# Where the products are added: onto the image in SBUF, or onto the output in DRAM

## The chip, the cores and the metric

The kernel runs on one core of a Trainium2 chip. The metric is device time in microseconds (us) of one execution; several runs are taken and their median is given. The core's engines are named as in the profile: PE is TensorE, DVE is VectorE, ACT is ScalarE, POOL is GpSimd and SP is SyncE, which only issues transfers.

## What is computed

The input has 160 images of 128 channels and 32 x 32 pixels in float32. Each is group-normalised, convolved 3 x 3 with weights that are quantised from U (five sets of weights; image number modulo 5 chooses the set), and added to the unnormalised image:

```python
def reference(x, L0_conv_U):            # x (160, 128, 32, 32), U (5, 128*128*9)
    beta, alpha = U.max(), U.min()
    s1 = (beta - alpha) / 3.0
    v1 = s1 * floor(U / s1)
    s2 = s1 / 5.0
    v2 = s2 * floor((U - v1) / s2)
    w = (v1 + v2).reshape(128 * 5, 128, 3, 3)
    g = x.reshape(160, 32, 4, 32, 32)   # 32 groups of 4 channels
    n = ((g - mean(g)) / sqrt(var(g) + 1e-5)).reshape(x.shape)
    act = grouped_conv(n.reshape(32, 5 * 128, 32, 32), w, groups=5, pad=1)
    return x + act.reshape(x.shape)
```

An image is 512 KB: 128 partitions (channels) with one row of 4 KB (1024 pixels) each.

## The kernel before

**Images and buffers.** The images are worked through set by set, 32 of one set after another. Two neighbouring images make a chunk of 1 MB (`NB = 2`), and a ring of ten chunks (`CHUNKS = 10`, tile `xt`) holds them in SBUF. `load(c)` brings a chunk in on SyncE's queue.

**Work on one image.** ACT or DVE measures it (`measure`, L377 and L384 on ACT), five images make a group whose means and variances are finished by small matmuls and a few short instructions (`ngm`, `twice`, `rstd`). Most images, 120, are "combined": DVE and POOL form sums and differences of neighbouring columns (`v`, lines 829, 836, 817 and 850), ACT scales them to float16 (`vh`, L879), and DVE forms the remainder (`vl`, L885). The 33 "plain" ones and a few at the start go through `z`, `hi` and `lo` instead. These are the last readers of the image in `xt`, but for its own addition at the end. PE then multiplies (L929, L984), with ACT and DVE exchanging partial sums (`leave` L1021, `pairs` L1030 and L1032), and leaves the products of an image in a pair of PSUM banks (`eo`, two buffers).

**The addition.** `residual(i)` ends an image, in one of two ways. By hand (`by_hand`: the first three images, the last four, and every tenth from 24 to 154) DVE adds `eo` onto the image in SBUF (L1073). For the other 139, ACT copies `eo` into one of three buffers `sum` (L1056), and `accumulate(i)` lets POOL issue a transfer that adds `sum` onto the image (L1079):

```python
self.nc.gpsimd.dma_start(self.image(i), self.sum.pop(i), accum_op=ALU.add)
```

When both images of a chunk are complete, SyncE stores the chunk (L1084). The next load into that buffer waits for that store. The last four images are stored one by one (L1075, L1066).

**The order of work.** Nearly all of it stands in a timetable, `steady`. Each step becomes a job with an engine, a cost and the jobs it needs; `Timetable.run` simulates the engines, picks for DVE and ACT the job that is due first, and the instructions are emitted in the order of the simulated starts. The order on PE is given, but for small matmuls that are slipped in. Stores and loads are jobs of an engine "queue" that takes 10 us each; they are emitted on SyncE's queue where the timetable starts them, and SyncE works through its queue in order: a transfer that has to wait holds up all that stand behind it. The same is true of POOL, whose queue holds the `v`, `z`, powers and accumulates.

Of the kernel before, what the change touches and what calls it, by code (L numbers as in the profile page):

```python
# [11 lines left out]
ALU = mybir.AluOpType  # L12
# [9 lines left out]
NB = 2  # L22
LAST = 4
# [23 lines left out]
class Timetable:  # L47
# [15 lines left out]
    def add(self, kind, engine, cost, emit, needs=(), **kw):  # L63
        job = Job(kind, engine, cost, emit, [n for n in needs if n is not None], **kw)
        self.jobs.append(job)
        place = {"tensor": self.tensor, "small": self.small, "beside": self.beside}
        place.get(engine, self.others).append(job)
        return job
# [452 lines left out]
class Main:  # L521
# [22 lines left out]


    CHUNKS = 10
    STEADY = 7
    BY_VECTOR = (8, 10, 11, 14, 19, 24, 29, 34)
    PLAIN = (9, 13, 17, *(22 + 9 * k + d for k in range(15) for d in (0, 4)))
# [11 lines left out]
    def __init__(self, tc, ctx, keep, x, u, out):  # L561
        self.tc = tc
        nc = self.nc = tc.nc
        self.imgs, C, self.H, self.W = x.shape
        P = self.P = nc.NUM_PARTITIONS
        assert C == P and self.H * self.W == 1024
        self.per_set = self.imgs // N_SETS
        self.xv = x.rearrange("(b n) c h w -> n c b (h w)", n=N_SETS)
        self.ov = out.rearrange("(b n) c h w -> n c b (h w)", n=N_SETS)
        self.uv = u.rearrange("n (o i k) -> n o i k", o=C, k=TAPS)  # L570

        def pool(name, bufs, **kw):
            return ctx.enter_context(tc.tile_pool(name=name, bufs=bufs, **kw))

        self.const = pool("const", 1)
        self.qpool = pool("quant", 1)
        self.wpool = pool("weights", 2)
        self.upool = pool("u", 1)
        self.xpool = pool("x", self.CHUNKS)
        self.zpool = pool("z", 2)  # L580
        self.parts = pool("parts", 4)
        self.rows = pool("rows", 4)
        self.wide = pool("wide", 3)
        self.wide_parts = pool("wide_parts", 4)
        self.evac = pool("evac", 2)
        self.sums = pool("sums", 3)
        self.unread = pool("unread", 1)
        self.small = pool("small", 5)
        self.ps_eo = pool("ps_eo", 2, space=PSUM)
        ps_m = pool("ps_m", 1, space=PSUM)  # L590
        ps_small = pool("ps_small", 1, space=PSUM)
        self.steps = Steps(nc, keep)

        self.m1a, self.m1b, self.m2_ps = (
            ps_m.tile([P, self.H // 2, self.W], F32, tag=name, name=name)
            for name in ("m1a", "m1b", "m2")
        )
        self.pair = [self.m1a, self.m2_ps]

        small = ps_small.tile([P, 512], F32, tag="small", name="small")  # L600
        self.pt, self.pg = small[:, : ROW * P].rearrange("p (k o) -> p k o", k=ROW), small[:, ROW * P :]
        self.chunks, self.z, self.hi, self.v, self.eo, self.m2 = {}, {}, {}, {}, {}, {}
        self.sum = {}
        self.turn_of = {}
        turn = 1
        for i in range(self.FIRST, self.imgs):
            if not self.plain(i):
                self.turn_of[i], turn = turn, 1 - turn
        self.tables, self.wts, self.across = {}, {}, {}
        self.columns = []  # L610

        cuts = [0, 2, 4, 8, 12, 16, *range(20, self.imgs + 1, 5)]
        self.groups = [range(a, b) for a, b in zip(cuts, cuts[1:])]
        self.group_of = {i: k for k, g in enumerate(self.groups) for i in g}
        self.stats = {}
# [432 lines left out]
    def residual(self, i):  # L1048

        nc = self.nc  # L1050
        eo = self.eo.pop(i)
        del self.hi[i]
        n, b = self.place(i)
        if not self.by_hand(i):
            self.sum[i] = self.sums.tile([self.P, 1024], F32, tag="sum", name=f"sum{i}")
            nc.scalar.copy(self.as_banks(i, self.sum[i]), self.flat(i, eo))  # L1056
            return
        xj = self.image(i)
        if i == self.imgs - 1:
            image, banks = self.as_banks(i, xj), self.flat(i, eo)  # L1060
            for a, quarters in ((0, (slice(0, 512),)), (1, (slice(0, 256), slice(256, 512)))):
                for h, q in enumerate(quarters):
                    nc.vector.tensor_add(image[:, a, q], banks[:, a, q], image[:, a, q])
                    if a == 1:
                        half = slice(h * 512, h * 512 + 512)
                        nc.sync.dma_start(self.ov[n, :, b, half], xj[:, half])  # L1066
            return
        image = self.as_banks(i, xj)
        if eo is self.pair:
            for a in range(2):  # L1070
                nc.vector.tensor_add(image[:, a], self.bank(eo, a), image[:, a])
        else:
            nc.vector.tensor_add(image, self.flat(i, eo), image)  # L1073
        if i >= self.imgs - LAST:
            nc.sync.dma_start(self.ov[n, :, b], xj)  # L1075

    def accumulate(self, i):
        if i in self.sum:
            self.nc.gpsimd.dma_start(self.image(i), self.sum.pop(i), accum_op=ALU.add)  # L1079

    def store(self, i):
        if 0 <= i < self.imgs - LAST and i % NB == NB - 1:
            n, b = self.place(i)
            self.nc.sync.dma_start(  # L1084
                self.ov[n, :, b - NB + 1 : b + 1, :], self.chunks[i // NB]
            )

    def run(self):
        nc, P = self.nc, self.P
# [126 lines left out]
        self.steps.choose()  # L1216
        for c in range(6, self.CHUNKS):
            self.load(c)
        for i in range(self.FIRST):
# [26 lines left out]
            self.residual(j)  # L1246
        self.steady(12, self.CHUNKS)

    def steady(self, measured, loaded):

        nc, imgs, first = self.nc, self.imgs, self.FIRST
        self.vector_engine = nc.vector.engine
        table = Timetable()
        add = table.add
        images = range(first, imgs)


        main, m1, m2, at, t = {}, {}, {}, {}, 0.0
# [3 lines left out]
        chain = [i for i in images if not self.plain(i)]  # L1262
# [27 lines left out]
        wide, beside, high, low, left, pairs, out, whole = ({} for _ in range(8))  # L1290
# [37 lines left out]


        stores, loads = {}, {}  # L1330
        for c in range(imgs // NB):
            if (c + 1) * NB <= imgs - LAST:
                stores[c] = add("store", "queue", 10.0, lambda c=c: self.store(c * NB + 1), (
                    [whole.get(c * NB + j) for j in range(NB)]
                ))
            if c >= loaded:
                loads[c] = add("load", "queue", 10.0, lambda c=c: self.load(c), (stores.get(c - self.CHUNKS),))


        combs = [i for i in images if self.combined(i)]  # L1340
        for n, i in enumerate(combs):
            if n >= 3:
                for job in (wide[i], beside[i]):
                    job.after(low[combs[n - 3]])
            if n >= 4:
                high[i].after(main[combs[n - 4]][1])
        plains = [i for i in images if self.plain(i) or i == 6]
        for a, b in zip(plains, plains[1:]):
            beside[b].after(low[a])
            high[b].after(main[a][1])  # L1350
        for n, i in enumerate(chain):
            if i in low and n >= 4:
                low[i].after(main[chain[n - 4]][1])
            if n >= 1 and i > first + 1:
                m2[i].after(left[chain[n - 1]])
            if n >= 2 and i > first + 1:
                m1[i].after(pairs.get(chain[n - 2]))
            if n >= 3:
                left[i].after(pairs.get(chain[n - 2]))
            if i in m2:  # L1360
                m2[i].after(low.get(i))
                main[i][0].after(pairs[i])
            if n and i in low and chain[n - 1] in pairs:
                pairs[chain[n - 1]].after(low[i])
        for i in images:
            if self.plain(i):
                main[i][0].after(low[i])
            user = main[i][0] if self.plain(i) else pairs.get(i)
            if user and i - 2 in out:
                user.after(out[i - 2])  # L1370
            if i - 3 in out:
                out[i].after(whole[i - 3])


        last_ve = None
# [1 line left out]
        for g, group in enumerate(self.groups):  # L1377
# [3 lines left out]
            for i in group:  # L1381
                if i < measured:
                    continue
                load = loads.get(i // NB)
# [27 lines left out]
        for n in range(1, N_SETS):  # L1412
# [3 lines left out]
            if n > 1:  # L1416
                load = add("load u", "queue", 0.1, lambda n=n: self.load_set(n), (last_rest,), ready=at[use - 40])
# [11 lines left out]
            for k, (kind, cost, gen) in enumerate(steps):  # L1429
                ready = start + (end - start) * k / len(steps)  # L1430
                job = add("step", kind, cost, lambda gen=gen: next(gen), (last,), ready=ready, late=ready + 6.0)
# [19 lines left out]
        for job in done:  # L1451
            for other in job.with_it:
                before = self.before_last()
# [58 lines left out]
```

## Time and profile before

| | |
|---|---|
| runs | 985.06, 990.72, 983.9 us; median 985.06 |
| profiled execution: own time / span | 983.48 / 981.7 us |
| PE busy | 938.0 us (96%) |
| DVE, ACT, POOL busy | 921.0 (94%), 852.4 (87%), 517.8 us (53%) |
| loads (1 MB each) | 78, median 7.6 us from issue to landing |
| stores (1 MB each) | 78, median 5.7 us |
| accumulates (512 KB each) | 139, 0.898 us of POOL each, median 6.8 us to landing (4.5 to 12.2) |
| DMA engines | 48.1% loads and stores, 39.7% accumulates |
| HBM | 89.19 MB read, 83.89 MB written |

An engine's busy time is the sum of its instructions' durations; idle time of an engine costs something only if another one waits for it. The DMA shares are the time that packets of a queue took, as a share of the 16 DMA engines' time over the span. "To landing" is from a transfer's issue to its end. In the views, a bracket or an arrow `<-` names what released an engine that had been idle.

### The profile page before, as it was taken

The page shows a single profiled execution, that of the slowest core. Times are in us where ns is not written, and L with a number is a line of the kernel's source. Part 1 is how long each engine was busy: PE and PEld are TensorE (multiplying, and loading weights), DVE is VectorE, ACT ScalarE, POOL GpSimd, SP SyncE. Part 2 cuts the span into 40 slices and gives each one's busy share as a digit, 9 for nine tenths or more (in the row PEclk, how much of TensorE's full clock was granted, in tenths as well). Part 3 has the DMA queues.
Part 4 walks back from the last instruction along what each step waited for, and adds up shares of the span by engine and source line. Part 5 has one row for each costly group of instructions (what it writes and reads, how often), then busy time and mean ns, then how long its engine had stood idle before and what let it go on. Part 6 is the DMA issues. An engine that isn't in the chain of part 4 may idle for free.

```text
span 981.7 us, 13015 instructions
## 1 busy us (share of the span) xinstructions
PE 938.0 (96%) x4514; PEld 442.2 (45%) x4514; DVE 921.0 (94%) x1175; ACT 852.4 (87%) x1118; POOL 517.8 (53%) x495
## 2 busy tenths in 40 slices
PE   2889999989999999999999999999999999999996
PEld 1434444444444444444444444444444444444443
DVE  7999999989999999899999999999999898978985
ACT  5779989869899997999999899998999999999651
POOL 4234655635575456465545557455655556455540
PEclk9999999999999999999999999999999999999999
DMA  9526999897999989999999889899999999897765
GB/s 354 219 86 195 239 265 291 229 283 211 260 286 271 263 254 241 277 269 263 254 319 268 241 235 275 242 278 306 249 277 257 257 255 283 250 299 218 182 166 196
DMA packets 65403, 246.89 MB, mean 252 GB/s; under 512 B 5040, under 2 KB 5040, under 8 KB 65328
## 3 DMA queue, kind: packets, MB, share of 16 engines
q1 hardware_dynamic: 45312, 173.09, 48.1%
q0 software_dynamic: 20016, 72.88, 39.7%
q8 instruction: 37, 0.61, 0.2%
q14 instruction: 38, 0.31, 0.1%
HBM read 89.19 MB, written 83.89 MB: 176 GB/s over the span
## 4 chain that ended last, share of the span: by engine, by line
PE 44%; DVE 31%; DMA 8%; issue 7%; ACT 6%; POOL 3%; SPq 0%; DVEq 0%; POOLq 0%; ACTq 0%
PE eo L984 15%; PE eo L929 13%; DVE vl L885 8%; PE m L984 7%; DVE v L829 5%; PE m1b L984 4%; PE m1a L984 4%; DMA xt<-in_x_dram 3%; DVE v L836 3%; DVE eo L1032 3%; DVE eo L1030 3%; DMA xt<-sum 3%; DVE lo L892 2%; ACT vh L879 2%; DMA out_dram<-xt 1%
## 5 line engine op out<-in xcount | busy, mean ns | idle before, releaser
L885 DVE SCALAR_TENSOR_TENSOR vl<-v,rstd,vh 128x2048 f16<-128x2048 f32 x120 | 286.3, 2386 | 23.5 <-ACT vh L879 23.2
L984 PE MATMUL eo<-vh,wt 128*128 128x512 f16 x720 | 269.5, 374 | 0.3 <-DVE eo L1032 0.2
L984 PE MATMUL eo<-vl,wt 128*128 128x512 f16 x720 | 269.6, 374 | 0.0
L879 ACT ACTIVATE vh<-v,rstd 128x2048 f16<-128x2048 f32 x120 | 239.0, 1995 | 23.1 <-POOL v L850 10.8
L817 POOL TENSOR_SCALAR v<-xt,ngm 128x64 f32<-128x64 f32 x120 | 129.6, 1080 | 212.8 <-issue 114.1
L984 PEld LDWEIGHTS <-across 128*128 128x128 f16 x1440 | 140.9, 98 | 172.0 <-issue 9.6
L984 PEld LDWEIGHTS <-wt 128*128 128x128 f16 x1488 | 145.2, 100 | 160.3 <-DVE rows L914 1.8
L929 PEld LDWEIGHTS <-wt 128*128 128x128 f16 x1368 | 134.0, 99 | 156.8 <-DVE eo L1032 3.3
L929 PE MATMUL eo<-hi,wt 128*128 128x496 f16 (+3 forms) x702 | 186.9, 377 | 4.8 <-DVE eo L1032 2.6
L377 ACT ACTIVATE junk<-xt 128x1024 uint8<-128x1024 f32 x152 | 160.5, 1056 | 26.5 <-DMA xt<-in_x_dram 24.9
L384 ACT ACTIVATE junk<-xt,mv 128x1024 uint8<-128x1024 f32 x152 | 174.4, 1148 | 2.8
L929 PE MATMUL eo<-lo,wt 128*128 128x496 f16 (+2 forms) x630 | 166.6, 375 | 0.0
L1079 POOL DMA_DIRECT2D xt<-sum x139 | 123.0, 898 | 78.5 <-ACT sum L1056 50.4
L1056 ACT COPY sum<-eo 128x1024 f32<-128x1024 f32 x139 | 148.3, 1067 | 16.8 <-PE eo L984 10.4
L850 POOL TENSOR_TENSOR v<-xt 128x512 f32<-128x512 f32 x120 | 155.6, 1297 | 0.0
L829 DVE TENSOR_TENSOR v<-xt 128x960 f32<-128x960 f32 x120 | 145.1, 1209 | 0.1
L984 PE MATMUL m<-vl,across 128*128 128x512 f16 x360 | 134.8, 375 | 4.4 <-DVE vl L885 4.4
L984 PE MATMUL m<-vh,across 128*128 128x512 f16 x360 | 134.9, 375 | 2.4 <-ACT m L1021 2.4
L856 POOL TENSOR_SCALAR z<-xt,ngm,rstd 128x1024 f32<-128x1024 f32 x33 | 60.8, 1841 | 65.0 <-DVE vl L885 16.9
L836 DVE SCALAR_TENSOR_TENSOR v<-xt,twice 128x512 f32<-128x512 f32 x120 | 91.3, 761 | 0.0
L1021 ACT ACTIVATE m<-m 128x512 f32<-128x512 f32 x124 | 73.5, 593 | 19.7 <-PE m L984 13.7
L422 POOL TENSOR_TENSOR rstd<-ve,mhalf 128x5 f32<-128x5 f32 (+2 forms) x34 | 54.3, 1598 | 54.2 <-DVE v L829 34.0
(143 smaller groups left out, 1001.3 us busy)
## 6 DMA issues: line engine op xcount, KB each, us to landing
xt<-in_x_dram SPq DMA_DIRECT2D x78, 1024.0 KB, 7.6
out_dram<-xt SPq DMA_DIRECT2D x78, 1024.0 KB, 5.7
xt<-sum POOLq DMA_DIRECT2D x139, 512.0 KB, 6.8
u<-in_L_conv_U_dram SPq DMA_DIRECT2D x4, 576.0 KB, 6.0
xt<-in_x_dram SPq DMA_DIRECT2D x4, 512.0 KB, 10.1
range<-in_L_conv_U_dram SPq DMA_DIRECT2D x3, 576.0 KB, 8.3
out_dram<-xt SPq DMA_DIRECT2D x3, 512.0 KB, 3.0
u<-in_L_conv_U_dram SPq DMA_DIRECT2D x2, 288.0 KB, 3.1
```

Source lines behind the costliest of these rows:

```text
L377: self.nc.scalar.activation(junk, image, ACTF.Copy, scale=-1.0 / image.shape[1], accum_out=self.mv[:, j, 0:1],)
L384: self.nc.scalar.activation(junk, image, ACTF.Square, bias=self.mv[:, j, 0:1], accum_out=self.mv[:, j, 1:2],)
L817: return self.nc.gpsimd.tensor_scalar(self.view(self.v[i], 0, (512 + W // 2 - 1, 2), (W // 2, H)), self.view(self.image(i), 1, (W - 3, 2), ...
L829: nc.vector.tensor_tensor(self.view(v, 1, (511, 2), (half, H), (1, half - 1)), self.view(x, 1, (1, 2), (W, H), (2, half - 1)), self.view(x ...
L836: nc.vector.scalar_tensor_tensor(v[:, 1024:1536], even, st.twice[:, j], odd, ALU.add, ALU.add)
L850: return [self.outer_columns(i), self.nc.gpsimd.tensor_sub(self.v[i][:, 1536:], odd, even)]
L879: self.nc.scalar.mul(vh, self.v[i], st.rstd[:, j])
L885: yield self.nc.vector.scalar_tensor_tensor(vl, self.v[i], st.rstd[:, j], self.hi[i], ALU.mult, ALU.subtract)
L929: nc.tensor.matmul(self.bank(target, a)[:, first:end, c0:c1], self.wts[n, col][:, k, :], tile[:, s0 : s0 + 2 * (end - first) - 1 : 2, c0 + ...
L984: self.nc.tensor.matmul(out, weights, moving, start=start and j == 0, stop=False, skip_group_check=True)
L1056: nc.scalar.copy(self.as_banks(i, self.sum[i]), self.flat(i, eo))
L1079: self.nc.gpsimd.dma_start(self.image(i), self.sum.pop(i), accum_op=ALU.add)
```

## The change

Each image that isn't summed by hand is stored to the output unchanged, as soon as it is loaded (`store_input`): a whole chunk at once, or one image where the other is summed by hand. `accumulate(i)` then adds the products onto that place of the output in DRAM, after the store has landed. A load into a buffer of the ring waits for the last readers of the old images and for their early store, and no longer for an accumulate and a store behind it. Images by hand are added in SBUF as before and stored one by one. The timetable counts 14 us for a load or store instead of 10; the four new constants `WIDE, HIGHS, ROWS, SUMS` have the values that stood in the code before.

```diff
     CHUNKS = 10
+    LANDING = 14.0
+    WIDE, HIGHS, ROWS, SUMS = 3, 4, 4, 3
...
         else:
             nc.vector.tensor_add(image, self.flat(i, eo), image)
-        if i >= self.imgs - LAST:
-            nc.sync.dma_start(self.ov[n, :, b], xj)
+        self.store(i)
 
     def accumulate(self, i):
-        if i in self.sum:
-            self.nc.gpsimd.dma_start(self.image(i), self.sum.pop(i), accum_op=ALU.add)
+        n, b = self.place(i)
+        added = self.nc.gpsimd.dma_start(self.ov[n, :, b], self.sum.pop(i), accum_op=ALU.add)
+        self.after(added, self.stored[i].ins)
 
     def store(self, i):
-        if 0 <= i < self.imgs - LAST and i % NB == NB - 1:
-            n, b = self.place(i)
-            self.nc.sync.dma_start(
-                self.ov[n, :, b - NB + 1 : b + 1, :], self.chunks[i // NB]
-            )
+        n, b = self.place(i)
+        return self.nc.sync.dma_start(self.ov[n, :, b], self.image(i))
+
+    def store_input(self, c):
+        images = [i for i in range(c * NB, c * NB + NB) if not self.by_hand(i)]
+        if len(images) == NB:
+            n, b = self.place(images[0])
+            stored = self.nc.sync.dma_start(self.ov[n, :, b : b + NB, :], self.chunks[c])
+            self.stored.update((i, stored) for i in images)
+            return
+        self.stored.update((i, self.store(i)) for i in images)
...
         stores, loads = {}, {}
+        def readers(i):
+            found = [beside.get(i), wide.get(i)]
+            return found + [out[i]] if i in out and self.by_hand(i) else found
         for c in range(imgs // NB):
-            if (c + 1) * NB <= imgs - LAST:
-                stores[c] = add("store", "queue", 10.0, lambda c=c: self.store(c * NB + 1), (
-                    [whole.get(c * NB + j) for j in range(NB)]
+            both, before = (range(k * NB, k * NB + NB) for k in (c, c - self.CHUNKS))
+            if c >= loaded:
+                loads[c] = add("load", "queue", self.LANDING, lambda c=c: self.load(c), (
+                    [stores.get(c - self.CHUNKS), *(j for i in before for j in readers(i))]
                 ))
-            if c >= loaded:
-                loads[c] = add("load", "queue", 10.0, lambda c=c: self.load(c), (stores.get(c - self.CHUNKS),))
+            if not all(self.by_hand(i) for i in both):
+                stores[c] = add(
+                    "store", "queue", self.LANDING, lambda c=c: self.store_input(c),
+                    (loads.get(c), loads.get(c + 1)), ready=6.0 * c if c < loaded else 0.0,
+                )
+            for i in both:
+                if not self.by_hand(i):
+                    whole[i].after(stores[c])
```

## The prediction

> **What bounds the kernel now.** I read the busy shares first, then stretches of the span, then the queues.
>
> ```profile
> PE 938.0 (96%) x4514; PEld 442.2 (45%) x4514; DVE 921.0 (94%) x1175; ACT 852.4 (87%) x1118; POOL 517.8 (53%) x495
> ```
>
> TensorE is busy for 938.0 of 981.7 us, so 43.7 us is all that a change which takes no matmul away can give back. The table of stretches says where those are.
>
> ```profile
> 0.00:25.00 25.00, 6.23 (x20) 3.43 (x21) 19.70 (x45) 12.95 (x24) 10.48 (x26) 1.00 0.94 355
> ...
> 200.00:250.00 50.00, 45.65 (x221) 21.53 (x222) 44.67 (x56) 40.36 (x53) 25.70 (x24) 1.00 0.87 243
> ...
> 400.00:450.00 50.00, 47.42 (x227) 21.96 (x225) 47.80 (x55) 47.58 (x65) 25.13 (x22) 1.00 0.92 257
> ...
> 700.00:750.00 50.00, 50.00 (x243) 23.67 (x242) 48.74 (x60) 47.89 (x63) 29.67 (x26) 1.00 0.97 264
> ```
>
> The first busy time in a row is PE's, the last three columns are granted clock, DMA share and GB/s. Before 75 us PE idles 25.4 us, after 960 us 8.1 us: start and end, in instructions that the change leaves alone. From 75 to 960 us the rows add up to 874.4 busy of 885, so **10.6 us is the whole prize in the steady part**. The last column but one is the warning: the DMA engines are 0.92 to 0.97 busy beside a full PE.
>
> Next, who waits for transfers: all waits, then the DMA queue's own.
>
> ```profile
> ACT junk L377 <- DMA xt<-in_x_dram: 24.9, 8, 8.2
> SPq L1084 <- DMA xt<-sum: 476.0, 75, 15.8
> SPq L635 <- DMA out_dram<-xt: 338.8, 56, 11.1
> ```
>
> SyncE's queue spends 476 us ahead of stores (L1084), held by accumulates, and 339 us ahead of loads (L635), held by stores. ScalarE feels it where it measures a new image (L377): 24.9 us, of which 14.9 after the start (another view has 6 such waits for L635). The chain of waits shows the worst one.
>
> ```profile
> 196.33 6.64 DMA xt<-sum
> ...
> 203.03 0.38 SPq L1084
> ...
> 203.52 9.71 DMA xt<-in_x_dram
> ...
> 213.31 0.07 ACT junk L377
> ```
>
> A load, kept until an accumulate had landed, lets ACT idle 6.67 us up to 213.31. PE loses 2.69 us between 210 and 225 us (4.37 + 4.09 + 3.85 busy of 15). The next worst, 4.10 us of ACT at 393.5, precedes PE gaps of 0.84, 0.62 and 0.90 us between 402 and 408: 2.36 us. The other four late loads, 0.5 to 1.8 us each, have no PE gap to their name. So late loads explain **2.69 + 2.36 = 5.05 us** of the 10.6. The rest belongs to the order on VectorE: 1.31 us at 201 behind a sum by hand (L1073), 1.78 us at 597 behind a vl that a 2.53 us L829 made late.
>
> **What the change removes.** A load into a buffer no longer waits for accumulate and store of its old images, but for their last readers and a store done long since. Readers run ahead: the last L829 (image 159) is at 953.3 us, the last copy into a sum (L1056, image 155) at 956.2. Accumulates run at (957.6 - 74.8) / 152 images = 5.81 us an image, so reading leads the copy by about 4 x 5.81 = 23 us (estimate). Copy 1.07, accumulate 6.8 and store 5.7 us to landing followed; a buffer comes free some 23 + 13.6 = 37 us sooner. A chunk with a hand-summed image keeps its buffer for 23 us + 1.2 + 3.0 (a 512 KB store's landing) and gains about 37 - 27 = 10 us. Both exceed the worst steady wait, 6.67 us. Gain: 5.05 us. The cover is those 10 us; without it up to 5.05 comes back.
>
> **What it adds on SyncE.** The same number of loads, and 16 more store issues, since a chunk with one hand image goes out as two 512 KB stores: 62 + 35 + 2 instead of 78 + 3 + 2. 16 x 0.38 = 6 us of a queue that waits most of the time: nothing. Each store now waits for its load (median 7.6 us to landing), and behind it stand the next loads, hand stores and the weight set. In the built order the next load usually precedes the store, and a chunk has 2 x 5.81 = 11.6 us; 7.6 + 0.8 fits even in series. Without cover a load slips by 7.6 us, inside the 10 to 37. The first weight load (issued at 43.1 us before) now stands behind hand stores whose sums end at 54 us: landing near 54.3 + 6 = 60, and its first user on VectorE runs at 74.9. Nothing.
>
> **What it adds on GpSimd.** The 139 issues of 0.898 us stay. Each waits for its image's store as well; behind it wait the combinations (L817, L850), then ACT's vh, then vl. Stores go out some 18 images early, so the wait is over except at the start, where the first three accumulates now stand behind z of image 9 (88.4 us before) instead of being issued at 74.8, 81.0 and 89.6. The fourth copy (97.0) needs the first of them landed: 89.7 + 6.8 = 96.5. Nothing, up to 1 us.
>
> **The cost that decides: an accumulate whose target is DRAM.** The trace has none.
>
> ```profile
> q1 hardware_dynamic: 45312, 173.09, 48.1%
> q0 software_dynamic: 20016, 72.88, 39.7%
> ```
>
> q0 is the accumulates: 0.397 x 981.7 / 139 = 2.80 us of all 16 engines each, or 350 ns per 4 KB row (8 rows an engine). q1 is loads and stores: 0.481 x 981.7 / 173.09 MB = 2.73 us a MB, 179 ns per row. So an accumulate costs 1.96 copies, as if it were paid for reading two rows. The queue's rates near the end, where transfers stand alone, agree (GB/s in 40 slices of 890 to 930 us):
>
> ```profile
> GB/s 262 242 246 410 418 426 356 94 217 201 29 115 406 397 131 0 193 201 160 201 201 266 430 401 45 0 131 197 197 0 229 410 401 74 197 197 66 16 66 205
> ```
>
> Accumulates alone 193 to 205, copies alone 397 to 430. In DRAM a row costs at best one copy, 179 ns (the two reads overlap, coming from two memories), at worst 350 + 179 = 529 ns (the read from DRAM comes on top). I take 350: loads and stores show DRAM as quick as SBUF in either direction, so nothing says that the second read gets dearer. Per image the engines then spend 2.86 (load and store, 1 MB) + 0.91 x 2.80 (139 of 153 images) = 5.40 of 5.81 us, 93% as in the rows above: unchanged. Break-even is (5.81 - 2.86) / 0.91 = 3.24 us an accumulate, **405 ns a row, only 16% above my value**. At 179 ns the load falls to 72%, worth nothing more, since PE bounds.
>
> The Trainium skill ("Collectives: The Full Stack", the section on the bandwidth ceiling) puts the half rate of an adding transfer down to its two source reads on one read ring, 62.28 against 32.35 GB/s; the 1.96 above agrees, and by that rule the sum would stay as it is. Against the change speaks "DMA: Bandwidth & Descriptors" (section on the anatomy of one DMA): the write receipt dominates a transfer's fixed time and HBM is the slowest target. By it an accumulate would land later; its figure of up to 2 us under load (section on latency) would make 6.8 into 8.8 us, which no run here shows yet.
>
> **Sum.** 983.5 (own time of the profiled execution, span 981.7) - 5.05 = 978.4. The median of the runs shown lies 1.6 us above that execution, so **980.0 us**.
>
> **Rivals.**
> *DMA becomes the bound* (slower): above 405 ns a row the engines need more than 5.81 us an image, sums are freed late, ACT's copies wait, PE follows. At the middle of 350 and 529, 440 ns: 2.86 + 0.91 x 3.52 = 6.06 us, +0.25 x 152 images = 39 us, and nothing gained: 1024. At 529: 6.71 us, +0.90 x 152 = 137: 1122. For it: the thin margin. Against: 1.96 copies.
> *Landings grow* (slower): three sum buffers give 3 x 5.81 = 17.4 us from copy to copy; 1.07 copy, some 3.7 until GpSimd issues (92.6 to 96.3 in one case) and 6.8 landing leave 5.8. SyncE now queues load, load, store together, where before it waited, so an accumulate meets more traffic. It decides above 12.6 us; at 13.5 the cycle is 18.3 / 3 = 6.09, and if half the images are hit, 0.28 x 76 = 21: 1006. Against: the maximum is 12.2 now.
> *Nothing is won*: VectorE is 94% busy and the timetable moves many of its and ACT's steps, so removed gaps may be replaced by gaps like that at 597: 985.
> *All 10.6 us are closed* by a better order: 974.4, faster by just over 1%.
>
> **How the numbers follow.** Forecast 0.36 (its own range 974 to 984), nothing won 0.14, all closed 0.12, DMA bound 0.24, landings 0.14. About 1% is what a measurement of this kernel can tell from no change: below 975.2 lie all of the third and 0.03 of the forecast, 0.15; above 994.9 the two slower ones, 0.38; between them 0.47. The range runs from 973 to 1040, past the centre of the DMA case; about 0.05 lies below and 0.13 above.
>
> **What would show it.** Right: ACT's waits at L377 for loads shrink from 14.9 us to under 3 in the steady part, SyncE's waits for accumulates are gone, PE's idle from 75 to 960 us is near 5.5 us, q0's share stays at 38 to 42%, HBM reads and writes rise by 72.9 MB each. Wrong: q0 above 46% with ACT's copies waiting for DMA; accumulates landing beyond 12 us; or PE gaps at vl and eo as many as before with no load behind them.

## The result, and the profile after

The changed kernel takes 989.58 us (median of 20 runs, 988.29 to 990.94), the kernel before 988.17 us (20 runs beside them, 983.23 to 1000.65). The ratio is 1.0009 with a 95% interval of 0.999 to 1.0027: no difference that can be measured. The forecast, 980.0 us, was a gain of half a per cent; there is none, though the time lies in the range. Two things stand out: the runs of the changed kernel lie within 2.7 us and those of the one before within 17 us, and the execution of before that the prediction was worked from (983.48 us) was one of that kernel's fast ones.

The profiled execution of the changed kernel took 988.58 us, its span is 986.9. From its page, busy times, queues, memory and issues (the last column of an issue is the median time to landing):

```profile
PE 937.3 (95%) x4514; PEld 442.6 (45%) x4514; DVE 916.7 (93%) x1175; ACT 854.2 (87%) x1118; POOL 518.1 (52%) x495
...
q1 hardware_dynamic: 45568, 173.09, 47.7%
q0 software_dynamic: 20016, 72.88, 39.7%
...
HBM read 89.19 MB, written 156.76 MB: 249 GB/s over the span
...
xt<-in_x_dram SPq DMA_DIRECT2D x78, 1024.0 KB, 9.9
out_dram<-sum POOLq DMA_DIRECT2D x139, 512.0 KB, 8.8
out_dram<-xt SPq DMA_DIRECT2D x62, 1024.0 KB, 12.1
```

TensorE does the same work. q0, the accumulates, takes the share that it took before: an accumulate onto DRAM costs 0.397 x 986.9 / 139 = 2.82 us of all engines, 352 ns a row. All transfers land later: loads 9.9 us after 7.6, accumulates 8.8 after 6.8, stores 12.1 after 5.7.

The stretches tell where the time went. Before, in two stretches (columns: window, length, busy time and count of PE, PEld, DVE, ACT, POOL; then granted clock, DMA share, GB/s):

```profile
75.00:250.00 175.00, 170.27 (x826) 80.50 (x825) 168.22 (x227) 153.50 (x201) 93.37 (x85) 1.00 0.89 248
250.00:960.00 710.00, 704.18 (x3400) 332.05 (x3399) 674.41 (x806) 645.91 (x836) 396.37 (x355) 1.00 0.92 258
```

After, the first of them in parts, then both:

```profile
75.00:100.00 25.00, 20.09 (x97) 9.46 (x96) 19.31 (x30) 16.18 (x23) 8.78 (x10) 1.00 1.04 381
100.00:150.00 50.00, 48.91 (x231) 22.82 (x230) 47.16 (x69) 49.72 (x69) 24.56 (x25) 0.97 1.04 326
150.00:200.00 50.00, 43.74 (x206) 20.12 (x205) 42.01 (x56) 42.84 (x62) 21.94 (x21) 0.97 0.91 274
...
75.00:250.00 175.00, 160.62 (x764) 75.08 (x763) 156.96 (x218) 152.00 (x206) 80.09 (x79) 0.98 0.99 303
250.00:960.00 710.00, 708.05 (x3429) 335.52 (x3429) 677.23 (x811) 643.95 (x826) 408.04 (x360) 1.00 0.89 243
```

Count TensorE's matmuls. From 250 to 960 us the changed kernel does 3429 where the one before did 3400: 29 more, 6.0 us at 0.207 us each: 3.9 us because PE idles 1.95 us there and not 5.82, the rest because a matmul takes a little less in the mean (0.2065 us, not 0.2071). From 75 to 250 us it does 764 where the one before did 826: 62 fewer, 12.8 us. Its idle time there is 14.38 us after 4.73, and its matmuls are slower too (0.210 us each, not 0.206), for the clock in the last columns is below 1 in two of the parts. The DMA share is 1.04 in both stretches from 75 to 150 us: all 16 engines are full. So the late loads after 250 us were removed, as forecast, and in these two executions the start lost more than that gave.

Who waits for transfers, all waits first, then SyncE's queue (total, times, longest):

```profile
ACT junk L377 <- DMA xt<-in_x_dram: 15.6, 3, 7.8
...
PE m L986 <- ACT m L1023: 9.4, 2, 4.9
...
ACT sum L1058 <- DMA out_dram<-sum: 8.0, 2, 7.2
```

```profile
SPq L1094 <- DMA xt<-in_x_dram: 228.3, 35, 13.6
...
SPq L637 <- DMA out_dram<-xt: 42.1, 18, 6.3
```

SyncE no longer waits for an accumulate; its stores (L1094) now wait for their loads. Of ACT's three waits for a load two are in the first microseconds, as before; the third, 6.0 us, and a wait of 7.2 us for a sum buffer (L1058) are new. Both are in the full stretch. The chain of waits has them:

```profile
88.70 9.37 DMA out_dram<-sum
98.15 1.01 ACT sum L1058
...
126.69 22.48 DMA xt<-in_x_dram
...
150.04 15.59 DMA xt<-in_x_dram
165.71 1.16 ACT junk L377 x2
```

POOL issues the first accumulate at 88.70 us (at 74.84 in the kernel before). It needs 9.37 us; ACT's copy into its buffer, the fourth of all copies, waits for it from 90.95 us on, and PE for ACT. Later a load needs 22.48 us (126.69 to 149.17); SyncE holds the store of that chunk (149.18) until it has landed, and the next load behind that store; it lands at 165.6 and the measurement waits. The copy, and PE's idle times behind the two waits:

```profile
98.15 1.01 ACT L1058 COPY sum<-eo 128x1024 f32<-128x1024 f32 x1 [7.20 <-DMA out_dram<-sum]
...
99.71 0.50 PE L986 MATMUL m<-vh,across 128*128 128x512 f16 x1 [4.91 <-ACT m L1023]
...
171.47 0.58 PE L986 MATMUL m<-vh,across 128*128 128x512 f16 x1 [4.50 <-ACT m L1023]
```

With those that follow the second (0.42 at 172.5, 1.35 at 177.5) they are 11.2 of the 14.38 us: 4.9 behind the copy, 6.3 behind the late load.

What fills the engines is seen in the transfers of 60 to 110 us, after and then before:

```profile
DMA packets 4023, 15.41 MB, mean 308 GB/s; under 512 B 270, under 2 KB 270, under 8 KB 4019
...
out_dram<-xt SPq DMA_DIRECT2D x10, 1024.0 KB, 17.2
xt<-in_x_dram SPq DMA_DIRECT2D x6, 1024.0 KB, 13.9
```

```profile
DMA packets 2628, 10.01 MB, mean 200 GB/s; under 512 B 192, under 2 KB 192, under 8 KB 2624
...
out_dram<-xt SPq DMA_DIRECT2D x4, 1024.0 KB, 4.0
xt<-in_x_dram SPq DMA_DIRECT2D x3, 1024.0 KB, 5.9
```

The chunks that were loaded ahead of the timetable are all stored at once, as soon as the timetable runs, and since buffers come free sooner, loads run ahead as well: ten 1 MB stores and six loads instead of four and three. These bytes are not more in the end, they are only moved forward; but they meet an engine budget of 93% and take long to drain. Whether full engines are what costs is asked below.

### The profile page after: what moved, and what is told of

Read it like the earlier page. It is cut to its first block, busy times and chain, and to the rows that moved or that the text cites. A ratio compares the mean times of both kernels' runs of the same rounds, so it can differ in the third digit from the quotient of the medians.

```text
span 986.9 us, 12939 instructions
## 1 busy us (share of the span) xinstructions
PE 937.3 (95%) x4514; PEld 442.6 (45%) x4514; DVE 916.7 (93%) x1175; ACT 854.2 (87%) x1118; POOL 518.1 (52%) x495
## 3 DMA queue, kind: packets, MB, share of 16 engines
q0 software_dynamic: 20016, 72.88, 39.7%
HBM read 89.19 MB, written 156.76 MB: 249 GB/s over the span
## 4 chain that ended last, share of the span: by engine, by line
PE 63%; DVE 19%; ACT 7%; DMA 5%; issue 4%; POOL 1%; SPq 0%; POOLq 0%; ACTq 0%; DVEq 0%
PE eo L986 22%; PE eo L931 18%; PE m L986 11%; PE m1b L986 5%; PE m1a L986 5%; DVE vl L887 5%; DMA xt<-in_x_dram 4%; DVE v L831 3%; ACT vh L881 2%; ACT junk L377 2%; DVE eo L1034 1%; DVE v L838 1%; DVE eo L1032 1%; DVE lo L894 1%; ACT junk L384 1%
## 5 line engine op out<-in xcount | busy, mean ns | idle before, releaser
L887 DVE SCALAR_TENSOR_TENSOR vl<-v,rstd,vh 128x2048 f16<-128x2048 f32 x120 | 290.6, 2423 | 26.4 <-ACT vh L881 26.1
L1058 ACT COPY sum<-eo 128x1024 f32<-128x1024 f32 x139 | 148.4, 1068 | 34.0 <-PE eo L986 18.4
L377 ACT ACTIVATE junk<-xt 128x1024 uint8<-128x1024 f32 x152 | 160.5, 1056 | 17.3 <-DMA xt<-in_x_dram 15.6
L1081 POOL DMA_DIRECT2D out_dram<-sum x139 | 122.7, 895 | 79.2 <-ACT sum L1058 74.5
L852 POOL TENSOR_TENSOR v<-xt 128x512 f32<-128x512 f32 x120 | 151.6, 1263 | 0.0
L831 DVE TENSOR_TENSOR v<-xt 128x960 f32<-128x960 f32 x120 | 141.8, 1182 | 0.2
L422 POOL TENSOR_TENSOR rstd<-ve,mhalf 128x5 f32<-128x5 f32 (+2 forms) x34 | 57.3, 1686 | 63.0 <-DVE v L831 28.1
## 6 DMA issues: line engine op xcount, KB each, us to landing
out_dram<-xt SPq DMA_DIRECT2D x62, 1024.0 KB, 12.1
```

Of the source, the lines that this page charges most:

```text
L377: self.nc.scalar.activation(junk, image, ACTF.Copy, scale=-1.0 / image.shape[1], accum_out=self.mv[:, j, 0:1],)
L831: nc.vector.tensor_tensor(self.view(v, 1, (511, 2), (half, H), (1, half - 1)), self.view(x, 1, (1, 2), (W, H), (2, half - 1)), self.view(x ...
L852: return [self.outer_columns(i), self.nc.gpsimd.tensor_sub(self.v[i][:, 1536:], odd, even)]
L887: yield self.nc.vector.scalar_tensor_tensor(vl, self.v[i], st.rstd[:, j], self.hi[i], ALU.mult, ALU.subtract)
L1081: added = self.nc.gpsimd.dma_start(self.ov[n, :, b], self.sum.pop(i), accum_op=ALU.add)
```

## The experiments

The theory from here on, the burst: the steady mechanism works as forecast, and what takes the gain back is the one-time backlog from 66 us on, made by early stores and early loads. Rivals: three sum buffers are too few now that accumulates land later; the new order of the timetable (14 us for a transfer instead of 10) made the gaps; and, for the gain, that it comes from loads being early rather than from a shorter chain of transfers. The ratios are to the kernel before, run beside on the same chip, with 95% intervals. "PE idle" is from 75 to 250 us / from 250 to 960 us, in the profiled execution.

| kernel | median us | ratio | PE idle us |
|---|---|---|---|
| before | 988.17 | 1 | 4.73 / 5.82 |
| after | 989.58 | 1.0009 [0.999, 1.0027] | 14.38 / 1.95 |
| e1_idle | 978.11 | 0.9915 [0.9894, 0.9936] | 4.46 / 2.28 |
| e2_jit | 985.49 | 0.998 [0.9964, 0.9996] | 4.78 / 7.52 |
| e3_sums4 | 992.65 | 1.0061 [1.0042, 1.008] | 17.23 / 1.99 |
| e4_before14 | 983.51 | 0.9972 [0.9956, 0.9988] | 5.29 / 6.02 |
| e5_late | 982.37 | 0.9942 [0.9921, 0.9963] | 5.81 / 1.86 |
| e6_idle_late | 975.01 | 0.9867 [0.9845, 0.9889] | 1.42 / 1.84 |
| e7_idle_no34 | 979.67 | 0.9917 [0.9895, 0.9938] | 7.59 / 2.34 |
| e8_idle_10 | 983.03 | 0.9947 [0.9927, 0.9968] | 4.97 / 4.89 |
| e9_chain | 987.65 | 1.0016 [0.9983, 1.0048] | 4.46 / 7.84 |
| e10_jit_late | 977.02 | 0.9898 [0.9857, 0.994] | 3.94 / 1.88 |
| e11_idle_late_s4 | 973.76 | 0.9872 [0.9831, 0.9914] | 1.44 / 1.83 |

**e1_idle: the same stores, put where the DMA engines idle.** Between 36 and 55 us almost nothing is transferred. The stores of the nine preloaded chunks are issued there, behind the second weight load; the steady timetable has store jobs for later chunks only.

```diff
         for c in range(6, self.CHUNKS):
             self.load(c)
+        self.load_set(1)
+        for c in range(1, self.CHUNKS):
+            self.store_input(c)
...
             if i == 2:
-                self.load_set(1)
...
-            if not all(self.by_hand(i) for i in both):
+            if c >= loaded and not all(self.by_hand(i) for i in both):
...
-                if not self.by_hand(i):
+                if not self.by_hand(i) and c in stores:
                     whole[i].after(stores[c])
```

> The changed kernel, with the early stores of the nine preloaded chunks issued right after their loads, in the stretch from about 43 to 75 us in which the DMA engines are nearly idle, instead of between 66 and 100 us. Theory A (the loss is a burst at the start: stores of preloaded chunks, loads and first accumulates together fill the DMA engines from 70 to 180 us, SyncE's queue in order passes the delay on): PE's idle time from 75 to 250 us falls from 14.4 to 5 us or less, the time is about 9 us below the changed kernel, near 980, ratio to the kernel before 0.991. Theory B (the timetable's new order on DVE and ACT makes the gaps, whatever the transfers do): the order hardly moves here, so 988 to 990. Theory C (accumulates onto DRAM land later and three sum buffers are too few, all the way): landings stay near 8.8 us and copies go on waiting, 986 to 990.

Measured: 978.11 us, 0.85% faster than before. The window of the changed kernel at 45 to 50 us, then those of this kernel:

```profile
45.00:50.00 5.00, 4.66 (x28) 2.25 (x27) 4.72 (x12) 3.49 (x8) 0.64 (x4) 1.00 0.00 0
```

```profile
45.00:50.00 5.00, 4.65 (x28) 2.26 (x27) 4.72 (x12) 3.69 (x8) 0.53 (x3) 1.00 0.96 354
...
75.00:250.00 175.00, 170.54 (x821) 80.53 (x819) 167.17 (x227) 162.04 (x217) 89.46 (x84) 0.99 0.96 278
250.00:960.00 710.00, 707.72 (x3427) 335.42 (x3426) 677.57 (x811) 639.53 (x822) 406.86 (x355) 1.00 0.88 240
```

The DMA share goes from nothing to full in that stretch while the compute engines' busy times hardly move, and 57 of the 62 missing matmuls are back. So what the changed kernel loses is lost at the start: 0.94% by the ratios (9 us), 11.5 us by the medians. But the place of these stores (and of one weight load) isn't all that differs. By the last lines of the edit the first accumulates no longer wait for a store's job in the timetable, so POOL issues them earlier. The first ones, in the changed kernel and here:

```profile
88.70 2.89 POOL L1081 DMA_DIRECT2D out_dram<-sum  x3
```

```profile
78.58 1.11 POOL L1081 DMA_DIRECT2D out_dram<-sum  x1 [3.69 <-ACT m L1023]
```

The first lands no faster here, after 9.8 us, but at 88.4 us, before ACT comes to the fourth copy (91.5). And the DMA engines are as full here (share 1.02 to 1.04 from 80 to 130 us) while PE idles nothing in that time. So full engines are not a loss in themselves: what costs is a transfer that is issued late, or slowed, with work waiting for it.

**e2_jit: no early stores at all.** A store job waits until the chunk before it has been read, instead of running ahead.

```diff
-                    (loads.get(c), loads.get(c + 1)), ready=6.0 * c if c < loaded else 0.0,
+                    [loads.get(c), loads.get(c + 1), *(
+                        j for i in range((c - 1) * NB, (c - 1) * NB + NB) for j in readers(i)[:2]
+                    )],
```

> The changed kernel, with the early store of a chunk held back until the chunk before it has been read, so that stores follow the pace of the images from the start and are not bunched behind the loads. Theory A: the DMA share from 75 to 150 us falls from 1.04 to 0.95 or less, no copy waits for an accumulate, PE's idle from 75 to 250 us is 6 us or less, time near 981, ratio to the kernel before 0.992. Theory B: new gaps elsewhere, 987 to 991. Theory C: no change, 988 to 990.

Measured: 985.49 us. The start is mended (4.78 us idle) but the steady part is not: 7.52 us. There are new gaps (1.48 us at 407, 1.05 at 565, 2.27 at 622), stores land in 15.0 us and loads in 11.2. None of these gaps ends with a transfer: they wait for ACT and DVE. Whether early loads that meet held stores are behind them is taken up in e10. From 75 to 100 us the DMA engines are full here too (share 1.04), and PE idles nothing.

**e3_sums4: a fourth sum buffer**, `SUMS = 4` instead of 3, and nothing else.

> The changed kernel with four buffers for sums instead of three. Theory A: the copy that waited 7.2 us for the first accumulate waits no more and its PE gap of 4.9 us at 99.7 goes, but the late load at 165 us and its gaps (4.5 + 0.4 + 1.4 us) stay: about 5 us gained, ratio to the kernel before 0.996. Theory C: all gaps up to 250 us go, ratio 0.991. Theory B: the order is made anew, gains and losses of 3 us either way.

Measured: 992.65 us, slower than the changed kernel. The wait for a sum buffer shrinks from 7.2 to 1.2 us and PE's gap at 99.7 is gone, so that wait was understood. But the loads then land later than in the changed kernel, at 156.9 and 168.0 us where it was 149.2 and 165.6, and ACT waits for both:

```profile
156.95 1.06 ACT L377 ACTIVATE junk<-xt 128x1024 uint8<-128x1024 f32 x1 [4.86 <-DMA xt<-in_x_dram]
...
168.12 1.06 ACT L377 ACTIVATE junk<-xt 128x1024 uint8<-128x1024 f32 x1 [8.74 <-DMA xt<-in_x_dram]
```

and PE idles 12.19 us before its matmul at 173.88. A fourth buffer alone is no cure: without the first wait the loads pay. Why they land later was not followed.

**e4_before14: the new cost in the kernel before**, the jobs of loads and stores at 14 us instead of 10, the transfers as before.

> The kernel before, with nothing changed but the 14 us that its timetable counts for a load or store instead of 10: the new order of the work without the new transfers. Theory A: ratio to the kernel before 1.000, within 0.003, late loads as before. Theory B: 1.005 or more, with PE gaps before 250 us that no transfer explains.

Measured: 983.51 us, ratio 0.9972. The waits for loads are as before (26.1 us in 8 waits), so the other order alone is worth 0.3%. So counting 14 us does not make gaps, it helps, and it is a part of the change that the forecast's sum had not priced. It is not yet the whole order of the changed timetable, in which the accumulates also wait for their stores (the 88.70 us above).

**e5_late: loads held back, stores as in the changed kernel.** The load into a buffer also needs the third image after the buffer's first old one to be out, which keeps loads from running ahead.

```diff
-                    [stores.get(c - self.CHUNKS), *(j for i in before for j in readers(i))]
+                    [stores.get(c - self.CHUNKS), *(j for i in before for j in readers(i)),
+                     out.get((c - self.CHUNKS) * NB + 3)]
```

> The changed kernel, but a load into a buffer waits besides until the image two further on has been put out, about 35 us later than its readers allow: the early stores of the preloaded chunks stay where they are, the early loads among them go. Theory A1 (both loads and stores make the burst): the DMA share from 75 to 150 us falls below 1, the first accumulates land in 8 us or less, PE's idle from 75 to 250 us falls from 14.4 to 8 or less, but in the part after 250 us some late loads come back (idle 2 to 6 us); 983 to 988. Theory A2 (the stores alone do it): the 4.9 us gap near 99.7 us stays; 988 to 992.

Measured: 982.37 us. The sum wait stays (6.71 us, PE gap 3.34 us at 100.8), the late load at 165 us is gone. The expected signs came only in part: the engines stay full, and the first accumulate, issued at 89.7 us, still needs 9.5.

```profile
75.00:100.00 25.00, 22.43 (x109) 10.54 (x107) 20.02 (x31) 17.40 (x25) 8.89 (x10) 1.00 1.03 388
100.00:150.00 50.00, 48.79 (x229) 22.75 (x229) 47.43 (x69) 45.67 (x61) 25.54 (x25) 0.97 1.04 323
```

So the start has two losses. The late load goes when loads are held, 0.67% by the ratios, though the engines are no emptier; the sum wait stays as long as the first accumulate is issued this late. The late loads of the steady part, expected back, stayed away: 1.86 us of idle after 250 us.

**e6_idle_late: both**, e1's stores in the idle stretch and e5's hold on the loads.

> The kernel with the stores of the preloaded chunks in the idle stretch (978.1 us), with the same hold on the loads as the run with late loads. It takes away the early loads alone. If the gain in the steady part comes from loads that no longer wait (the forecast's mechanism): ACT waits for loads again in the steady part, 5 us or more in all, PE's idle from 250 to 960 us rises from 2.3 to 4 to 8 us, time 981 to 987. If it comes from the other order of the work: nothing moves, 977 to 980.

Measured: 975.01 us (974.37 to 976.12), ratio 0.9867. I had expected the steady part's late loads to return and a time of 981 to 987; they did not. The windows:

```profile
75.00:250.00 175.00, 173.58 (x844) 82.35 (x843) 172.64 (x234) 158.33 (x209) 96.72 (x88) 1.00 0.92 263
250.00:960.00 710.00, 708.16 (x3426) 334.89 (x3425) 677.20 (x807) 644.32 (x833) 387.43 (x352) 1.00 0.88 245
```

3.26 us of idle in 885, and no measurement waits for a load but those in the first microseconds. That loads come early is not what removed the late loads; that left the shorter chain, which e9 tests.

**e7_idle_no34: the gap of 2.34 us that e1 kept at 165.6.** I read it as VectorE's doing, since image 34 is one whose steps VectorE takes over (`BY_VECTOR`), and took 34 out of that list in e1's kernel.

> The kernel with the stores in the idle stretch, and image 34 measured by ACT instead of DVE. Its last large gap, 2.34 us of PE at 165.6 us, comes where that measurement (two instructions of 0.68 us and three short ones) stands ahead of the pairs that PE waits for, and a stretch of half the granted clock of 3.4 us follows. Theory: gap and clock dip go, 2 to 4 us gained, 974 to 976, ratio to the kernel before 0.988. Rival: ACT, 94% busy there, becomes late instead and it stays at 977 to 980.

Measured: 979.67 us, no faster. A gap of 2.52 us stays at 165.96 and others come (7.59 us idle in all). The edit missed what it aimed at: the measurement ahead of the gap in e1, at 162.4 us, is the seventh of VectorE's eight, that of image 29, and it still stands there in this run, at 162.8. The one that went is the eighth, image 34's, at 193.5 in e1. So the theory was not tested. In e1 the chain that leads to the gap (vh on ACT, then vl, v, that measurement and the pairs on DVE) has no transfer in it from 126 us on; in e6 the same measurement (160.6 us) has no gap behind it. By what means the gap goes there was not followed.

**e8_idle_10: the transfers without the new cost**, e1 with `LANDING = 10.0`.

> The kernel with the stores in the idle stretch, with 10 us instead of 14 counted for a load or store in the timetable. Tells how much the order of the work is worth: within 977 to 980 if the transfers set the result, 982 or more if the 14 us order the work well.

Measured: 983.03 us, ratio 0.9947. Against e1 the 14 us of the timetable are worth 0.32% by the ratios, 4.9 us by the medians. And this kernel is the nearest to what the forecast priced: the new transfers, the old cost, no loss at the start. By the ratio it gains 0.53%, 5.2 us; the forecast had 5.05. The traces do not bear that match out: its profile still has three late loads of 1.2 to 1.6 us (4.2 us, 14.9 before) and gaps from the order on VectorE of 1.97 us at 620 and 1.36 at 484, and PE's idle from 75 to 960 us is 9.86 us where it was 10.55. Its profiled execution (981.85) is only 1.6 us ahead of before's (983.48), itself 4.7 us below its median. As far as the traces go, the agreement with 5.05 is luck.

**e9_chain: transfers in series again.** In e6's kernel the hold on loads is replaced by a wait of the load for the landing of the old images' accumulates. It isn't needed for the data. The timetable sees only that they were issued, not when they land, as in the kernel before.

```diff
+            for i in range((c - self.CHUNKS) * NB, (c - self.CHUNKS) * NB + NB):
+                if i in self.added:
+                    self.after(loaded, self.added[i].ins)
...
-                     out.get((c - self.CHUNKS) * NB + 3)]
+                     *(whole.get(i) for i in before)]
```

> The kernel with early stores in the idle stretch and late loads (975.0 us), but the hold on a load is another one: it waits, as in the kernel before, until the accumulates of the old images in its buffer have landed, so that an accumulate and a load stand in series again on the chip (before: accumulate, store and load). The timetable counts nothing for the accumulate's landing, as before. If transfers in series, which the timetable doesn't see, are what made loads late in the kernel before: ACT waits for loads in the steady part again, 3 us or more after 75 us, and the time is 978 or more. If not: no waits and 974 to 977.

Measured: 987.65 us, ratio 1.0016: the whole gain is gone. Its waits of ACT, those of SyncE ahead of loads, and two of its instructions on ACT and PE:

```profile
ACT junk L377 <- DMA xt<-in_x_dram: 37.8, 14, 8.1
```

```profile
SPq L637 <- DMA out_dram<-sum: 651.2, 92, 17.4
```

```profile
346.01 1.06 ACT L377 ACTIVATE junk<-xt 128x1024 uint8<-128x1024 f32 x1 [5.00 <-DMA xt<-in_x_dram]
```

```profile
352.12 0.56 PE L409 MATMUL small<-dv,gavg 128*128 128x5 f32 x2 [5.48 <-DVE dv L438]
```

12 late loads besides the two of the start, and behind one of 5.00 us a PE gap of 5.48. So a chain of transfers that the timetable does not see makes loads late, and taking it away is what the change gains in the steady part. The jobs of the loads stand elsewhere in the timetable too, a rival that these waits make unlikely but do not exclude. The runs spread again, 985.68 to 994.11; but the chain alone does not make the spread, for e4 has all of it and its 12 runs lie within 4.0 us.

**e10_jit_late: e2 with the hold on loads.** It asks whether e2's later gaps came from early loads meeting held stores.

> Stores held back until the chunk before has been read, and loads held until the image two further on is out: no transfer of the new scheme is early any more, nothing is put into the idle stretch. With stores held back alone the start was mended (PE idle 4.8 us from 75 to 250 us), but the rest had 7.5 us of idle time. If those later gaps come from early loads that meet the held stores: they shrink to about 2 us and the time is 977 to 980. If they come from the order that held stores give the work: 984 to 987.

Measured: 977.02 us. Idle after 250 us falls from 7.52 to 1.88, as expected if early loads made the gaps. The hold also orders the work anew, and e2's gaps did not end with transfers, so which of the two it was isn't shown. Nothing is moved into the idle stretch here: a paced start is enough, 2 us from e6.

**e11_idle_late_s4: e6 with four sum buffers.**

> The best kernel so far (stores in the idle stretch, late loads; 975.0 us) with four buffers for sums. Copies wait 2.7 us for accumulates in it and PE idles 3.3 us from 75 to 960 us. If landings of 8.7 us on DRAM cost anything there: 1 to 2 us gained, 973 to 974. If the three buffers cover them: 974 to 977.

Measured: 973.76 us (973.42 to 975.37) beside e6's 975.01 (on another chip, ratios 0.9872 and 0.9867). Once the start is mended a fourth buffer is worth a microsecond at most. The landing of accumulates at 8.7 us, as in the changed kernel, costs nothing that can be measured in the steady part. This is the lowest median; by the ratios it and e6 are level, 1.3% ahead of the kernel before.

## Why the prediction was wrong

**Right in part: the mechanism of the steady part.** Loads late by a chain accumulate, store, load were named as the loss, at 5.05 us of PE. Such loads are gone after 250 us (PE idle 5.82 to 1.95), and e9 brings such a loss back by putting two transfers in series. But the 3.87 us are more than the 2.36 that the prediction gave to late loads there, and by e8 and e4 it takes both parts of the change: with the new transfers alone 4.2 of the 14.9 us of late loads stay and PE's idle hardly falls (10.55 to 9.86 us from 75 to 960), with the new cost alone the late loads all stay.

**Right: the cost that decides.** 350 ns a row for an accumulate onto DRAM was taken between 179 and 529; 352 was measured, q0's share stayed at 39.7%, and DMA as a bound of the whole run falls as a rival. This agrees with the two reads on one ring of the Trainium skill ("Collectives: The Full Stack", bandwidth ceiling), which states them for the add of a reduce-scatter and which the prediction weighed; the destination being in DRAM changes nothing of it here.

**Right in size by luck: landings.** They grew to 8.8 us in the median (16.5 at most), the very figure that the prediction had worked out for a target in DRAM, but not by that. From 890 to 930 us, where transfers stand nearly alone, it is 5.3 us in the median where it was 4.6, so the target makes 0.7. The rest goes with the number of other transfers under way. Counted in the traces after 250 us, an accumulate issued beside one, two or three others lands after 4.8, 6.8 and 8.9 us before and 5.5, 7.7 and 8.8 after; three or more were under way for 26 of 111 before and 54 of 112 after. After 250 us no copy waited for a landing; e11 bounds what it costs.

**Wrong: "What it adds on GpSimd", given "Nothing, up to 1 us".** This is the step that failed first. The prediction saw that the first three accumulates would stand behind z of image 9, and let the fourth copy, at 97.0 us, wait for the first to land at 96.5. But the copy at 97.0 is the fifth. The kernel before starts its copies into a sum at 68.94, 78.45, 85.47, 91.64 and 97.02 us:

```profile
91.64 0.99 ACT L1056 COPY sum<-eo 128x1024 f32<-128x1024 f32 x1
...
97.02 1.08 ACT L1056 COPY sum<-eo 128x1024 f32<-128x1024 f32 x1
```

With three buffers it is the fourth, at 91.64, that needs the first accumulate landed, so the prediction's own numbers made a wait of 4.9 us. Measured: ACT waits 7.20 us and PE 4.91. Of the 7.20, 2.6 come from a landing of 9.4 us instead of 6.8; the rest is the late issue, at 88.70. In e1 it is at 78.58, and no copy waits there, with a landing of 9.8.

**Wrong: "What it adds on SyncE", given "Nothing".** The working counted issues, and the order in which they stand, but not bytes. It had a budget for the steady pace, 5.40 of 5.81 us an image, and none for the stores and loads that are due at once when the timetable begins. Some 9 MB of early stores at 2.73 us a MB are 25 us of all engines; a slack of 7% in 5.81 us an image gives back 0.4 us an image, so this is not drained within a few images; the engines stayed full from 70 to 180 us. The sentence "a load slips by 7.6 us, inside the 10 to 37" met a load of 22.48 us, with a store and the next load held behind it: ACT waits 6.02 us, PE 6.3. e5, which holds the loads, is free of it.

Measured price of the two together: 9 to 11.5 us (e1). How it divides between the bytes of the stores and the late issue of the accumulates, no run shows.

**Wrong: the order was not priced in the sum.** The cost of 14 us moves instructions. The prediction let that open gaps in one rival (985) and close them all in another (974.4), but put it at nothing in its sum. It is worth 0.28% (e4) to 0.32% (e8).

By the ratios the parts add up: -0.53% for the transfers, -0.32% for the order, +0.94% for the start make +0.09%, the measured 1.0009. (The sum is exact because the three are steps between e8, e1 and the changed kernel; that the steps are those causes is what e4, e5 and e9 support.)

**The base.** The sum started from an execution of 983.48 us and a median of 985.06 of three; the median of 20 is 988.17. Against that, a gain of 5 us would have been 983. No trace shows an execution of the kernel before near its median, so what those lose beside the 10.6 us is not known.

**What would show it.** Of the signs that the prediction gave, the waits at L377 under 3 us, and PE's idle of 5.5 us from 75 to 960, failed (6.0 and 16.3 us), both by the start. HBM's written bytes rose by 72.87 MB as said; its read bytes did not rise.

**Open.** What makes the gap that e7 was after, and why a change to image 34 opens others; what makes e2's later gaps; what makes the runs of the kernel before spread; and how much of before's loss belongs to the store in its chain, since e9 has two transfers in series, not three.

## What to carry to other kernels

A transfer that is only moved earlier is not free. Multiply the bytes that become due at once by the time that a MB takes on all engines and divide by the slack of the steady pace: for up to that long transfers land later (here 25 us by 7%, some 360 us at the most; the engines were full for 110). Then ask which transfer has work waiting for it in that time, and what holds its issue back; full engines that nobody waits for cost nothing (e1, e2). Count buffers by the copies that take them, first to last, before saying which copy waits. A stretch where the engines idle can take such transfers. A static timetable that does not count the landing of a transfer makes late loads wherever transfers wait for each other in series; shortening the chain helped here, counting the landing was not tried. When one wait at the head of a backlog is removed, expect another to pay (e3).

## What the runs showed of the hardware

**An accumulate costs the same onto DRAM as onto SBUF**: 352 against 350 ns of a DMA engine for a row of 4 KB, and 0.7 us more to landing when it is alone.

**The profile's count of HBM reads does not grow when accumulates go to DRAM.** It is 89.19 MB before and after, while the bytes written rose by the 72.87 MB of the accumulates. So what an accumulate reads at its target does not show in that count.

**A short idle time of PE can halve its clock for about 3.4 us.** After its gap of 4.91 us, PE's granted clock in the changed kernel (the column behind the busy times):

```profile
99.70:101.00 1.30, 1.29 (x4) 0.55 (x4) 1.27 (x2) 1.30 (x3) 0.64 (x1) 0.55 1.07 290
101.00:102.00 1.00, 1.00 (x4) 0.30 (x2) 1.00 (x2) 1.00 (x2) 0.00 (x0) 0.50 1.02 274
...
103.00:104.00 1.00, 1.00 (x6) 0.45 (x5) 1.00 (x2) 1.00 (x3) 0.00 (x0) 0.88 1.10 291
```

Matmuls that otherwise start 0.21 us apart start 0.41 to 0.43 us apart there (100.00, 100.43, 100.84, 101.25). Two such stretches (here and at 171.5) make the 764 matmuls of 75 to 250 us dearer by 764 x (0.2102 - 0.2061) = 3.1 us: a gap costs more than its length. The Trainium skill ("TensorE: Matmul & The Clock Gate", Part 1) has the clock halved after an idle window of some 3.4 us, by a window that runs freely. The length of the slow stretch agrees, and longer gaps gave twice and four times that (6.83 us at 0.50 around e9's gap of 5.48 us, 13.65 around e3's of 12.19). The gap needed does not quite: e1's gap of 2.34 us was followed by a clock of 0.50 too, e7's of 2.52 us by none.
